# Turning three matrices per group by 32-row blocks through DRAM and VectorE in place of TensorE transposes

## The chip, the cores and the metric

The kernel runs on one core of a Trainium2 chip. The metric is the device time of one execution in microseconds (us). The kernel before takes 2581.26 us, the median of three runs that lie between 2580.55 and 2581.66 us.

## What is computed

The input is x, 128 batches of 128 nodes with 256 features each, in float32, and one 128x128 adjacency matrix. Four layers follow each other, and each has the same frame:

```
h = maximum(layernorm(x), 0)
x = x + layer(h)
```

- Layer 0 is a gated graph layer: `relu((A_in h + e_in)*sigmoid(g_in) + (A_out h + e_out)*sigmoid(g_out) + h*sigmoid(g_loop))`, with gates of one number per node. The kernel gathers the three terms in one 128x128 matrix per batch (`cmb`, the gated sum of A_in, A_out and the identity), which is then multiplied with h.
- Layer 1 is causal attention with one head: scores from h, an additive mask, softmax, product with the values.
- Layer 2 is three graph convolutions, 256 to 512 to 1024 to 256 features.
- Layer 3 is a graph convolution, a product to 512 features, a batch norm over all 128x128 rows, a product back to 256 features, and a second batch norm.

The batch norms need statistics of all rows, so the kernel makes two passes: layers 0 to 2 and the first half of layer 3 for all batches, then the rest of layer 3.

## The kernel before, in words

Four batches form a group (`G = 4`, 512 rows), and there are 32 groups (`NG`). A tile of a group has 128 partitions (the nodes) and the four batches side by side.

The layers are Python generators that yield between stages: `layer0`, `layer1`, `layer2`, `layer3`. The first pass is software-pipelined over groups. In turn g, layer 2 of group g (stream C), layer 1 of group g+1 (stream B), layer 0 of group g+2 (stream A) and layer 3 of group g-1 (stream D) are interleaved, with the norm that opens layer 1 of group g+2 as stream b and that of layer 3 of group g as stream d. The string `TURN` (line 837) says in which order the streams advance; `FINAL` (line 840) does so for the last turn, and `FILL` (line 850) for the start, in which group 0 is worked in halves. A scheduler then places the recorded instructions on the engines; each engine works through its own queue in order and waits where an operand is not there. Loads of x and stores of z go through the SyncE (SP) queue, which also works in order.

TensorE multiplies a stationary operand, contracted over partitions, so some matrices must be turned first. Three matrices of a group are turned by TensorE in the kernel before, each 128x128 block by a multiplication with the identity into PSUM and an eviction to SBUF:

- **cmb** of layer 0, four blocks: the transposes into `pc` on line 553, evicted by VectorE on line 555, used as stationary operand on line 561.
- **h** of layer 1, eight blocks: `turn` (lines 393 to 400), called on line 578, writes two PSUM tiles `pt`; ScalarE evicts the first and VectorE the second into `hT`. `sums` (line 412) then forms combinations of the quarters of hT, and the products of `seven` (line 460, a seven-product scheme for a two-by-two block multiplication) use hT and the sums as operands.
- **p**, the unnormalised softmax of layer 1, four blocks: ScalarE's exponentials on line 649, the transposes into `pp` on line 658, evicted by VectorE on line 660, used as stationary operand for `py` on line 666.

Group 0 and, for layer 0, group 1 take partly different paths at the start (halves, and gates by TensorE), which the change leaves on TensorE.

Of the kernel before, what the change touches and what calls it, by code (L numbers as in the profile page):

```python
# [8 lines left out]
FP = mybir.dt.float32  # L9
AF = mybir.ActivationFunctionType  # L10
ALU = mybir.AluOpType
# [4 lines left out]
P = 128  # L16
# [6 lines left out]
def kernel(  # L23
# [39 lines left out]
    nc = tc.nc  # L63
    B, N, D = x.shape
    G = 4
    NG = B // G
    T = G * N
    DC = D // P
# [13 lines left out]
    def bank(shape, name):  # L82
        return psum[-1].tile(shape, FP, tag="bank", name=name)
# [273 lines left out]
            whole[name] = w.tile(shape, FP, tag=tag, name=name, bufs=bufs)  # L357
        return whole[name]

    def norm(g, layer, bs=ALL):  # L360

        xt, n, tail = X[g], len(bs), f"{layer}_{g}_{bs[0]}"
        st = small.tile([P, n, 6], FP, tag="st", name=f"st{tail}")
        mv = small.tile([P, n, 2], FP, tag="mv", name=f"mv{tail}")
        for k, b in enumerate(bs):
            nc.vector.bn_stats(st[:, k, :], xt[:, b, :])  # L366
        for k in range(n):
            nc.vector.bn_aggr(mv[:, k, :], st[:, k, :])
        rs = small.tile([P, n], FP, tag="rs", name=f"rs{tail}")
        sh = small.tile([P, n], FP, tag="sh", name=f"sh{tail}")  # L370
        if n == G:
            nc.gpsimd.tensor_scalar(rs, mv[:, :, 1], LN_EPS, None, ALU.add)  # L372
            nc.gpsimd.tensor_tensor(rs, rs, nhalf[:, :n], ALU.pow)  # L373
            nc.gpsimd.tensor_scalar(sh, mv[:, :, 0], -1.0, None, ALU.mult)
            nc.gpsimd.tensor_tensor(sh, sh, rs, ALU.mult)  # L375
        else:
            inv_sqrt(rs, mv[:, :, 1], LN_EPS)
            nc.vector.scalar_tensor_tensor(sh, mv[:, :, 0], -1.0, rs, ALU.mult, ALU.mult)
        h = tile_of(g, bs, [P, G, D], "h", f"h{layer}_{g}", 3)
        for k, b in enumerate(bs):  # L380
            relu = nc.scalar.activation(  # L381
                h[:, b, :], xt[:, b, :], AF.Relu, bias=sh[:, k : k + 1], scale=rs[:, k : k + 1]
            )
            if (g, layer) == (1, 0):

                tc.keep_in_program_order(relu)
        return h

    def columns(dst, c, bs):

        return dst[:, c, bs[0] * P : (bs[-1] + 1) * P]

    def turn(dst, h, bs, name):

        for c in range(DC):
            pt = bank([P, len(bs), P], f"{name}_{c}")
            for k, b in enumerate(bs):
                nc.tensor.transpose(pt[:, k, :], h[:, b, c * P : (c + 1) * P], ident)
            evict = nc.vector.tensor_copy if c else nc.scalar.copy
            evict(columns(dst, c, bs), pt.rearrange("p b n -> p (b n)"))  # L400

    def mixed(dst, src, aT, name, evicts, bs=ALL):

# [91 lines left out]
    def layer0(g, bs=ALL):  # L495

        xt, n, tail = X[g], len(bs), f"{g}_{bs[0]}"
        h = norm(g, 0, bs)
        yield
        gl = small.tile([P, n, 3], FP, tag="gl", name=f"gl_{tail}")  # L500
        gate_bias = gb[:, None, :].to_broadcast([P, n, 3])
        if g < 2:

            hT = tile_of(g, bs, [P, DC, T], "dT", f"h0T_{g}", 2)
            turn(hT, h, bs, f"ph_{tail}")
            yield
            pl = bank([P, n, 3], f"pl_{tail}")
            for k, b in enumerate(bs):
                for c in range(DC):
                    nc.tensor.matmul(  # L510
                        pl[:, k, :], hT[:, c, b * P : (b + 1) * P], gwT[:, c, :],
                        start=(c == 0), stop=(c == DC - 1),
                    )
            nc.vector.tensor_tensor(gl, pl, gate_bias, ALU.add)
        else:
            gs = w.tile([P, D], FP, tag="gs", name=f"gs_{tail}", bufs=1)
            for k, b in enumerate(bs):
                for i in range(3):
                    nc.vector.scalar_tensor_tensor(  # L519
                        gs, h[:, b, :], 1.0, gw[:, i, :], ALU.mult, ALU.mult,  # L520
                        accum_out=gl[:, k, i : i + 1],
                    )
                if k == n // 2 - 1:
                    yield
            nc.vector.tensor_tensor(gl, gl, gate_bias, ALU.add)
        gt = small.tile([P, n, 3], FP, tag="gt", name=f"gt_{tail}")
        nc.scalar.activation(gt, gl, AF.Sigmoid)
        yield


        um = tile_of(g, bs, [P, 2, G, D], "um", f"m_{g}", 1)
        bias = um[:, 0]
        cmb, cmbT = (
            um[:, 1, 2 * k : 2 * k + 2, :].rearrange("p a (b n) -> p (a b) n", n=P) for k in range(2)
        )
        for k, b in enumerate(bs):
            nc.scalar.activation(cmb[:, b, :], ain, AF.Copy, scale=gt[:, k, 0:1])
            nc.vector.scalar_tensor_tensor(
                cmb[:, b, :], aout, gt[:, k, 1:2], cmb[:, b, :], ALU.mult, ALU.add
            )  # L540
            nc.vector.scalar_tensor_tensor(
                cmb[:, b, :], ident, gt[:, k, 2:3], cmb[:, b, :], ALU.mult, ALU.add
            )
        for k, b in enumerate(bs):
            nc.scalar.activation(bias[:, b, :], eb, AF.Copy, scale=gt[:, k, 0:1])
        yield
        for k, b in enumerate(bs):
            nc.vector.scalar_tensor_tensor(
                bias[:, b, :], oeb, gt[:, k, 1:2], bias[:, b, :], ALU.mult, ALU.add
            )  # L550
        pc = bank([P, n, P], f"pc_{tail}")
        for k, b in enumerate(bs):
            nc.tensor.transpose(pc[:, k, :], cmb[:, b, :], ident)
        mine = slice(bs[0], bs[-1] + 1)
        nc.vector.tensor_copy(cmbT[:, mine, :], pc)
        yield
        for q in range(bs[0] // 2, (bs[-1] + 1) // 2):
            pm = bank([P, 2, D], f"pm_{g}_{q}")
            for r in range(2):
                b = 2 * q + r  # L560
                nc.tensor.matmul(pm[:, r, :], cmbT[:, b, :], h[:, b, :], start=True, stop=True)  # L561
            half = slice(2 * q, 2 * q + 2)
            nc.vector.tensor_tensor(bias[:, half, :], pm, bias[:, half, :], ALU.add)
        yield
        nc.vector.scalar_tensor_tensor(
            xt[:, mine, :], bias[:, mine, :], 0.0, xt[:, mine, :], ALU.max, ALU.add
        )
        yield

    def layer1(g, bs=ALL):  # L570
# [1 line left out]

        xt, n, tail = X[g], len(bs), f"{g}_{bs[0]}"
        halves = range(bs[0] // 2, (bs[-1] + 1) // 2)
        h = norm(g, 1, bs)
        yield
        hT = tile_of(g, bs, [P, DC, T], "dT", f"hT_{g}", 2)
        turn(hT, h, bs, f"pt_{tail}")
        if n == G:
            ex = w.tile([P, 4, 1, T // 2], FP, tag="ex", name=f"hs_{g}", bufs=2)  # L580
            hs = sums(nc.vector, quarters_t(hT), ex, ex[:, 3])
        yield
# [62 lines left out]
        nmax = small.tile([P, n], FP, tag="nmax", name=f"nmax_{tail}")  # L645
        nc.vector.tensor_reduce(nmax, p, AX.X, ALU.max, negate=True)
        psumr = small.tile([P, n], FP, tag="psumr", name=f"psumr_{tail}")
        for k in range(n):
            nc.scalar.activation(
                p[:, k, :], p[:, k, :], AF.Exp, bias=nmax[:, k : k + 1],  # L650
                accum_out=psumr[:, k : k + 1],
            )
        rsum = small.tile([P, n], FP, tag="rsum", name=f"rsum_{tail}")
        nc.vector.reciprocal(rsum, psumr)
        yield
        pp = bank([P, n, P], f"pp_{tail}")
        for k in range(n):
            nc.tensor.transpose(pp[:, k, :], p[:, k, :], ident)
        pT = tile_of(g, bs, [P, G, P], "pT", f"pT_{g}", 1)[:, bs[0] : bs[-1] + 1, :]
        nc.vector.tensor_copy(pT, pp)  # L660
        yield
        for q in halves:
            py = bank([P, 2, D], f"py_{g}_{q}")
# [109 lines left out]
    def layer3(g):  # L773
# [16 lines left out]
        def put(ij, pb, other):  # L790
# [13 lines left out]
            if done.count(j) == 2:  # L804
                if g < LAST - 1:
                    for jj in range(2):
                        nc.vector.bn_stats(stats1[:, 2 * j + jj, g, :], z[j][:, jj, :])
                if g != LAST:
                    nc.sync.dma_start(Z[g][:, 2 * j : 2 * j + 2, :], z[j])

        if g < LAST:
            yield from seven(columns_by_half(gs, SETS["b"], 0), put, [P, 2, T // 2], f"pz_{g}")
            return
        for i, j in (0, 0), (1, 0), (0, 1), (1, 1):
            pb = bank([P, 2, T // 2], f"pz_{g}_{i}_{j}")
# [18 lines left out]

    TURN = "CCCBCCABBDABBCABBDDCBADCDDBDCCDBACBCCABCCACbBCBBCBCBBCBCBCdB"


    FINAL = "CCCCCCCCCCCCCCCCCCDCCCCDDdDDddDdDdDdddd"  # L840
    US = {}
    AHEAD = 3

# [18 lines left out]
        in_turn(at, KEPT)  # L862
    assert all(next(stream[k], k) == k for k in "acbdA")
    bs, ds = part(layer1, 1), stream["p"]
    next(bs)
    for g in range(NG):
        if g + AHEAD < NG:
            load_x(g + AHEAD)
# [253 lines left out]
```

## Time and profile before

| What | Value | Where it is read |
|---|---|---|
| time | 2581.26 us (2580.55 to 2581.66) | three runs |
| span of the profiled execution | 2581.1 us | page, first line |
| busy TensorE, VectorE, ScalarE, GpSimd | 2535.9, 1905.8, 1288.8, 288.9 us | page, part 1 |
| mean granted TensorE clock | 0.994 | table of cores |
| one turn of the first pass | 70.8 us | the timeline of TensorE: the same block returns every 70.8 us |
| DMA traffic in the first pass | about 31 GB/s, 9% of the engines' time | table of stretches |

The engine columns are busy times, so shares of the span of engines that work beside each other; they do not add up to the span. A TensorE instruction in the timeline overlaps the next one by its pipeline, so what a block of matmuls costs is read as the distance from its start to the start of the block behind it. Float32 matmuls appear as two records each.

### The profile page before, as it was taken

Reading aid. Unit: us, or ns where it says so; the run is one execution under the profiler, and the core shown is the slowest. Engines: PE = TensorE matmul, PEld = TensorE weight load, DVE = VectorE, ACT = ScalarE, POOL = GpSimd, SP = SyncE. Lnnn points to the kernel's source line nnn. Section 1 sums busy time; section 2 is a strip of 40 time slices with the busy share of each in tenths; the row PEclk is TensorE's granted clock in tenths of the full one; section 3 lists DMA queues with packets and bytes.
Section 4 is the critical chain, followed back from the end, with each engine's and each line's share of the span. In section 5 each row is a group of like instructions: output and inputs, shape, how many; then the busy total and the mean of one; then the engine's idle time right before and its main releaser. Section 6 shows DMA issues by size and latency. Waiting matters only on the chain.

```text
span 2581.1 us, 40737 instructions
## 1 busy us (share of the span) xinstructions
PE 2535.9 (98%) x15316; PEld 2293.4 (89%) x15316; DVE 1905.8 (74%) x4795; ACT 1288.8 (50%) x2577; POOL 288.9 (11%) x563
## 2 busy tenths in 40 slices
PE   7999999999999999999999999999999999999996
PEld 6999999999999999999999999999999999988875
DVE  7777777777777777777777777777777777658886
ACT  4545445444444554454444445544454444337766
POOL 1111111111111111011111111110111111000001
PEclk9999999999999999999999999999999999999998
DMA  4000000000000000000000000000100000025459
GB/s 134 15 34 33 34 34 27 24 34 34 34 26 25 34 34 34 34 34 17 34 33 34 33 22 29 34 34 33 34 25 25 34 25 25 25 104 212 173 192 386
DMA packets 49655, 143.05 MB, mean 55 GB/s; under 512 B 4258, under 2 KB 23220, under 8 KB 45492
## 3 DMA queue, kind: packets, MB, share of 16 engines
q1 hardware_dynamic: 42884, 117.33, 12.6%
q0 software_dynamic: 6432, 23.07, 2.5%
q8 instruction: 120, 1.97, 0.3%
q14 instruction: 75, 0.61, 0.1%
q10 hardware_dynamic: 144, 0.07, 0.0%
HBM read 73.48 MB, written 66.98 MB: 54 GB/s over the span
## 4 chain that ended last, share of the span: by engine, by line
PE 95%; ACT 2%; DVE 1%; DMA 1%; issue 0%; POOL 0%; SPq 0%; DVEq 0%; POOLq 0%
PE p_x L452 17%; PE p_x L435 9%; PE p_z L452 8%; PE pmu L407 4%; PE p_z L435 4%; PE p_y L452 4%; PE po_x L995 4%; PE pu_x L435 4%; PE pz_x L452 4%; PE pg L407 2%; PE pm L407 2%; PE ps L636 2%; PE pm L561 2%; PE p_y L435 2%; PE pr L766 2%; PE pqv_x L593 2%
## 5 line engine op out<-in xcount | busy, mean ns | idle before, releaser
L381 ACT ACTIVATE h<-x,sh,rs 128x256 f32<-128x256 f32 x512 | 269.0, 589 | 358.4 <-POOL sh L375 345.8
L452 PE MATMUL p_x<-uT,w 128*128 128x256 f32 x1024 | 242.2, 379 | 0.0
L738 ACT ACTIVATE h2T<-h2T 128x512 f32<-128x512 f32 x192 | 120.5, 627 | 229.9 <-DVE h2T L737 229.9
L452 PEld LDWEIGHTS p_x<-uT,w 128*128 128x128 f32 x1024 | 189.7, 190 | 23.1
L366 DVE BATCH_NORM_STATS2 st<-x 128x6 f32<-128x256 f32 x512 | 190.9, 414 | 2.3
L372 POOL TENSOR_SCALAR rs<-mv 128x4 f32<-128x4 f32 x124 | 29.9, 241 | 1350.0 <-ACT h2T L738 1061.0
L519 DVE SCALAR_TENSOR_TENSOR gs<-h,gw 128x256 f32<-128x256 f32 x360 | 150.4, 418 | 27.9 <-ACT h L381 22.6
L467 ACT COPY p_t<-p_x 128x512 f32<-128x512 f32 (+1 forms) x192 | 96.7, 504 | 109.9 <-PE p_x L452 102.8
L373 POOL TENSOR_TENSOR rs<-rs,nhalf 128x4 f32<-128x4 f32 x124 | 144.6, 1166 | 0.0
L407 PEld LDWEIGHTS pmu<-a2T,u 128*128 128x128 f32 x1024 | 119.3, 192 | 14.8 <-issue 14.8
L435 PEld LDWEIGHTS p_x<-w,h2T 128*128 128x128 f32 x1024 | 124.3, 192 | 3.3
L691 ACT ACTIVATE u<-u 128x512 f32<-128x512 f32 x93 | 58.6, 630 | 133.8 <-DVE u L690 133.8
L435 PE MATMUL p_x<-w,h2T 128*128 128x128 f32 x1024 | 124.6, 275 | 0.0
L452 PE MATMUL p_x<-us,w_s 128*128 128x256 f32 x512 | 121.2, 379 | 0.0
L452 PE MATMUL p_x<-uT,w_s 128*128 128x256 f32 x512 | 121.1, 379 | 0.0
L452 PE MATMUL p_y<-uT,w 128*128 128x256 f32 x512 | 121.0, 379 | 0.0
L452 PE MATMUL p_z<-us,w_s 128*128 128x256 f32 x512 | 121.0, 379 | 0.0
L452 PE MATMUL p_z<-us,w 128*128 128x256 f32 x512 | 120.9, 379 | 0.0
L407 PE MATMUL pmu<-a2T,u 128*128 128x128 f32 x1024 | 119.5, 275 | 0.0
L452 PEld LDWEIGHTS p_z<-us,w_s 128*128 128x128 f32 x512 | 97.3, 190 | 13.2
L452 PEld LDWEIGHTS p_z<-us,w 128*128 128x128 f32 x512 | 97.3, 190 | 13.2
L452 PEld LDWEIGHTS p_y<-uT,w 128*128 128x128 f32 x512 | 97.2, 190 | 13.2
(324 smaller groups left out, 6115.6 us busy)
## 6 DMA issues: line engine op xcount, KB each, us to landing
z<-zo SPq DMA_DIRECT2D x62, 512.0 KB, 2.6
zi<-z SPq DMA_DIRECT2D x31, 1024.0 KB, 4.9
x<-x POOLq DMA_DIRECT2D x32, 512.0 KB, 3.5
x<-in_x_dram SPq DMA_DIRECT2D x31, 512.0 KB, 4.0
out_dram<-x3i SPq DMA_DIRECT2D x30, 512.0 KB, 10.7
x3i<-x SPq DMA_DIRECT2D x20, 512.0 KB, 6.1
x3i<-x POOLq DMA_DIRECT2D x12, 512.0 KB, 8.8
w<-in_L_gnn_W_dram SPq DMA_DIRECT2D x1, 2048.0 KB
```

What stands on the lines that cost most here:

```text
L366: nc.vector.bn_stats(st[:, k, :], xt[:, b, :])
L373: nc.gpsimd.tensor_tensor(rs, rs, nhalf[:, :n], ALU.pow)
L381: relu = nc.scalar.activation(h[:, b, :], xt[:, b, :], AF.Relu, bias=sh[:, k : k + 1], scale=rs[:, k : k + 1])
L407: nc.tensor.matmul(pm[:, k, :], src[:, b, c * P : (c + 1) * P], aT, start=True, stop=True)
L435: nc.tensor.matmul(pb[:, rr, :], a_r[r][:, c, rr * P : (rr + 1) * P], b_r[r][:, c, :wide], start=(first and rr == 0 and c == 0), stop=(c = ...
L452: nc.tensor.matmul(pb[:, jj, :], b_r[r][:, c, at : at + P], a_r[r][:, c, :], start=(first and jj == 0 and c == 0), stop=(c == nk - 1), ski ...
L467: nc.scalar.copy(t, pb)
L519: nc.vector.scalar_tensor_tensor(gs, h[:, b, :], 1.0, gw[:, i, :], ALU.mult, ALU.mult, accum_out=gl[:, k, i : i + 1],)
L561: nc.tensor.matmul(pm[:, r, :], cmbT[:, b, :], h[:, b, :], start=True, stop=True)
L691: nc.scalar.activation(dst, dst, AF.Relu)
L738: nc.scalar.activation(dst, dst, AF.Relu)
L995: nc.tensor.matmul(pb, BW2R[r][:, c, :], a_r[r][:, c, :], start=(first and c == 0), stop=(c == FC // 2 - 1), skip_group_check=True,)
```

## The change

The three matrices are no longer turned by TensorE. A 128x128 block is seen as four by four blocks of 32x32. Turning it is an exchange of those blocks across the diagonal, and a turn inside each block. The exchange is done by DMA: four writes, one for each stripe of 32 partitions, put the blocks into a DRAM tile `home` in exchanged order, and one read brings them back (`swap`). The turn inside the blocks is one VectorE instruction over all blocks (`cut`).

So that each piece that travels is contiguous, the instruction that makes the matrix (ScalarE's relu for h, VectorE's last addition for cmb, ScalarE's exponential for p) writes it already in a blocked layout. The purpose is to take the transposes off TensorE's queue. Since an exchange takes longer than a transpose, the streams get more yields between making and using a turned matrix, and `TURN` is rewritten so that other work stands between them. The stores of z are moved behind the exchange reads of the turn in the SP queue (`follow`).

It applies to cmb of groups 2 to 31, and to h and p of groups 1 to 31.

```diff
@@ norm @@
         for k, b in enumerate(bs):
+            dst, src = h[:, b, :], xt[:, b, :]
+            if blocks:
+                dst = h.rearrange("p b d -> p (b d)").rearrange(
+                    "p (j k b r) -> p b j k r", j=P // 32, k=DC, b=G
+                )[:, b]
+                src = src.rearrange("p (k j r) -> p j k r", k=DC, j=P // 32)
             relu = nc.scalar.activation(
-                h[:, b, :], xt[:, b, :], AF.Relu, bias=sh[:, k : k + 1], scale=rs[:, k : k + 1]
+                dst, src, AF.Relu, bias=sh[:, k : k + 1], scale=rs[:, k : k + 1]
             )
...
+    def swap(blocks, name):
+        e = blocks.shape[1] // NQ
+        home = scratch.tile([NQ, Q, NQ, e], FP, name=name)
+        for i in range(NQ):
+            nc.sync.dma_start(
+                home[:, :, i, :].rearrange("j r e -> r j e"),
+                blocks[i * Q : (i + 1) * Q].rearrange("p (j e) -> p j e", j=NQ),
+            )
+        nc.sync.dma_start(blocks, home.rearrange("j r i e -> (j r) (i e)"))
+        fetched.append(nc.cur_bb.bb.instructions[-1].name)
+
+    def cut(dst, blocks, nb):
+        tc.keep_in_program_order(
+            nc.vector.transpose(
+                dst.rearrange("p (b i c) -> p b i c", b=nb, i=NQ),
+                blocks.rearrange("p (i b c) -> p b i c", i=NQ, b=nb),
+            )
+        )
@@ layer0 @@
-            nc.vector.scalar_tensor_tensor(
-                cmb[:, b, :], ident, gt[:, k, 2:3], cmb[:, b, :], ALU.mult, ALU.add
-            )
+            dst, one, now = cmb[:, b, :], ident, cmb[:, b, :]
+            if g >= 2:
+                dst = flatT.rearrange("p (j b r) -> p b j r", j=NQ, b=G)[:, b]
+                one, now = (a.rearrange("p (j r) -> p j r", j=NQ) for a in (one, now))
+            nc.vector.scalar_tensor_tensor(dst, one, gt[:, k, 2:3], now, ALU.mult, ALU.add)
+        if g >= 2:
+            swap(flatT, f"cc_{g}")
...
-        pc = bank([P, n, P], f"pc_{tail}")
-        for k, b in enumerate(bs):
-            nc.tensor.transpose(pc[:, k, :], cmb[:, b, :], ident)
         mine = slice(bs[0], bs[-1] + 1)
-        nc.vector.tensor_copy(cmbT[:, mine, :], pc)
+        if g >= 2:
+            yield
+            cut(cmb.rearrange("p b n -> p (b n)"), flatT, G)
+            cmbT = cmb
+        else:
...
@@ layer1 @@
-        h = norm(g, 1, bs)
+        h = norm(g, 1, bs, n == G)
+        if n == G:
+            blocks = h.rearrange("p b d -> p (b d)")
+            swap(blocks, f"hc_{g}")
         yield
         hT = tile_of(g, bs, [P, DC, T], "dT", f"hT_{g}", 2)
-        turn(hT, h, bs, f"pt_{tail}")
-        if n == G:
+        if n < G:
+            turn(hT, h, bs, f"pt_{tail}")
+        else:
+            cut(hT.rearrange("p c t -> p (c t)"), blocks, DC * G)
+            yield
             ex = w.tile([P, 4, 1, T // 2], FP, tag="ex", name=f"hs_{g}", bufs=2)
             hs = sums(nc.vector, quarters_t(hT), ex, ex[:, 3])
...
+        if n == G:
+            swap(flat_p, f"pc_{g}")
...
-        pp = bank([P, n, P], f"pp_{tail}")
-        for k in range(n):
-            nc.tensor.transpose(pp[:, k, :], p[:, k, :], ident)
-        pT = tile_of(g, bs, [P, G, P], "pT", f"pT_{g}", 1)[:, bs[0] : bs[-1] + 1, :]
-        nc.vector.tensor_copy(pT, pp)
+        if n == G:
+            cut(p.rearrange("p b s -> p (b s)"), flat_p, G)
+            pT = p
+        else:
...
@@ layer3 @@
-                if g != LAST:
-                    nc.sync.dma_start(Z[g][:, 2 * j : 2 * j + 2, :], z[j])
...
+            at = len(nc.cur_bb.bb.instructions)
+            for j in (1, 0):
+                nc.sync.dma_start(Z[g][:, 2 * j : 2 * j + 2, :], z[j])
+            for i in nc.cur_bb.bb.instructions[at:]:
+                for name in fetched[-2:]:
+                    follow(i, name)
+            yield
...
-    TURN = "CCCBCCABBDABBCABBDDCBADCDDBDCCDBACBCCABCCACbBCBBCBCBBCBCBCdB"
+    TURN = "CCBBCBCABCBBCABDBACBDDACDCADDCDCBDCADBCBACACbCBCBBCBBCBBCBCbBCd"
-    FINAL = "CCCCCCCCCCCCCCCCCCDCCCCDDdDDddDdDdDdddd"
+    FINAL = "CCCCCCCCCCCCCCCCCCDCCCCDDdDDddDdDdDDdddd"
...
-    next(bs)
+    for _ in range(2):
+        next(bs)
```

More of the change, by code (lines that the diff above doesn't have):

```diff
@@ L358, in tile_of, with norm @@
         return whole[name]
-    def norm(g, layer, bs=ALL):
+    def norm(g, layer, bs=ALL, blocks=False):
         xt, n, tail = X[g], len(bs), f"{layer}_{g}_{bs[0]}"
@@ L400, in turn, with follow @@
             evict(columns(dst, c, bs), pt.rearrange("p b n -> p (b n)"))
+    Q = 32
+    NQ = P // Q
+    fetched = []
+    def follow(i, name):
+        tc.add_manual_dep(
+            i, name,
+            mybir.DependencyInfo(mybir.DependencyClass.NoSync, mybir.DependencyReason.DATA),
+            reason="follow",
+        )
[15 more added lines that the diff above has]
+            )
+        )
     def mixed(dst, src, aT, name, evicts, bs=ALL):
@@ L535, in layer0 @@
         )
+        flatT = cmbT.rearrange("p b n -> p (b n)")
         for k, b in enumerate(bs):
@@ L550, in layer0 @@
             )
-        pc = bank([P, n, P], f"pc_{tail}")
-        for k, b in enumerate(bs):
-            nc.tensor.transpose(pc[:, k, :], cmb[:, b, :], ident)
         mine = slice(bs[0], bs[-1] + 1)
-        nc.vector.tensor_copy(cmbT[:, mine, :], pc)
+        if g >= 2:
[3 more added lines that the diff above has]
+        else:
+            pc = bank([P, n, P], f"pc_{tail}")
+            for k, b in enumerate(bs):
+                nc.tensor.transpose(pc[:, k, :], cmb[:, b, :], ident)
+            nc.vector.tensor_copy(cmbT[:, mine, :], pc)
         yield
@@ L647, in layer1 @@
         psumr = small.tile([P, n], FP, tag="psumr", name=f"psumr_{tail}")
+        pT = tile_of(g, bs, [P, G, P], "pT", f"pT_{g}", 1)[:, bs[0] : bs[-1] + 1, :]
+        flat_p = pT.rearrange("p b s -> p (b s)")
         for k in range(n):
+            dst, src = p[:, k, :], p[:, k, :]
+            if n == G:
+                dst = flat_p.rearrange("p (j b r) -> p b j r", j=NQ, b=G)[:, k]
+                src = src.rearrange("p (j r) -> p j r", j=NQ)
             nc.scalar.activation(
-                p[:, k, :], p[:, k, :], AF.Exp, bias=nmax[:, k : k + 1],
-                accum_out=psumr[:, k : k + 1],
-            )
+                dst, src, AF.Exp, bias=nmax[:, k : k + 1], accum_out=psumr[:, k : k + 1],
+            )
+        if n == G:
+            swap(flat_p, f"pc_{g}")
         rsum = small.tile([P, n], FP, tag="rsum", name=f"rsum_{tail}")
@@ L655, in layer1 @@
         yield
-        pp = bank([P, n, P], f"pp_{tail}")
-        for k in range(n):
-            nc.tensor.transpose(pp[:, k, :], p[:, k, :], ident)
-        pT = tile_of(g, bs, [P, G, P], "pT", f"pT_{g}", 1)[:, bs[0] : bs[-1] + 1, :]
-        nc.vector.tensor_copy(pT, pp)
+        if n == G:
+            cut(p.rearrange("p b s -> p (b s)"), flat_p, G)
+            pT = p
+        else:
+            pp = bank([P, n, P], f"pp_{tail}")
+            for k in range(n):
+                nc.tensor.transpose(pp[:, k, :], p[:, k, :], ident)
+            nc.vector.tensor_copy(pT, pp)
         yield
```

## The prediction

> **What bounds the kernel now.** I read the table of stretches first: how busy each engine is in one turn of the first pass, at what clock, with how much DMA. Three of its rows (length, then busy time and instructions of TensorE, its weight loads, VectorE, ScalarE, GpSimd, then clock, DMA share, GB/s):
>
> ```profile
> 978.80:1049.60 70.80, 70.80 (x440) 64.53 (x439) 52.77 (x138) 34.45 (x70) 8.68 (x17) 1.00 0.09 31
> 1049.60:1120.40 70.80, 70.80 (x440) 64.53 (x439) 52.78 (x138) 34.45 (x70) 8.68 (x17) 1.00 0.09 30
> 1120.40:1191.20 70.80, 70.80 (x440) 64.53 (x439) 52.77 (x138) 34.44 (x70) 8.69 (x17) 1.00 0.09 31
> ```
>
> TensorE fills every turn to the last hundredth at full clock, VectorE is idle for 18 us of it, ScalarE for 36 us, DMA nearly always. The page's chain of waits agrees for the whole span:
>
> ```profile
> PE 95%; ACT 2%; DVE 1%; DMA 1%; issue 0%; POOL 0%; SPq 0%; DVEq 0%; POOLq 0%
> ```
>
> So TensorE time removed in the steady state shortens the kernel one for one, as long as nothing that TensorE needs comes later than its turn in the queue. Busy time of a transpose is not its price, since neighbours overlap; the timeline of TensorE gives the price as the distance between starts:
>
> ```profile
> 1016.20 0.60 PE L658 MATMUL pp<-ident,p 128*128 128x128 f32 x4
> 1016.64 0.60 PE L553 MATMUL pc<-ident,m 128*128 128x128 f32 x4
> 1017.07 1.89 PE L452 MATMUL p_x<-us,w_s 128*128 128x256 f32 x8
> ...
> 1058.27 1.04 PE L398 MATMUL pt<-ident,h 128*128 128x128 f32 x8
> 1059.14 1.89 PE L452 MATMUL p_x<-us,w_s 128*128 128x256 f32 x8
> ```
>
> Four transposes of p and four of cmb take 1017.07-1016.20 = 0.87 us, eight of h 0.87 us, with no bracket of idle time behind any of them.
>
> [...]no turn by VectorE is in this trace. [...]a z store of 512 KB lands in 2.6 us, an x load of 512 KB in 4.1 us[...]. The trace shows the slowing after an even shorter gap, in the fill:
>
> ```profile
> 29.54 0.33 PE L398 MATMUL pt<-ident,h 128*128 128x128 f32 x1 [1.47 <-ACT h L381]
> 30.03 0.90 PE L398 MATMUL pt<-ident,h 128*128 128x128 f32 x3 [0.16 <-ACT h L381]
> 30.97 2.08 PE L612 MATMUL pqv<-hT,m_qk 128*128 128x256 f32 x4
> 32.84 1.27 PE L620 MATMUL pqv<-w_vo,hT 128*128 128x128 f32 x8
> 33.94 1.03 PE L612 MATMUL pqv<-hT,m_qk 128*128 128x256 f32 x4
> ```
>
> The same four records take 2.08 us at first and 1.03 us later. From 29.54 to 32.84 passed 3.3 us where 1.3 us of work at full rate and 0.2 us of waiting stood: 1.8 us lost.
>
> **What is removed.** h and p in 31 groups, 31 x (0.87+0.435) = 40.5 us, and cmb in 30 groups, 30 x 0.435 = 13.0 us: **-53.5 us**, 1.74 us a turn. With them go evictions of 0.69+0.69+0.68 us on VectorE and 0.59 us on ScalarE per turn.
>
> **What is added beside TensorE.** On VectorE one block turn of 128x1024 and two of 128x512. Nearest rows of those sizes: 1.23 us (the addition on L565) and 0.69 us (the eviction on L660), together 2.6 us, net +0.5 us in 18 us of idle time. At twice the price it is +3.2 us, still within it. ScalarE and VectorE write h, p and cmb in runs of 32 elements; I take the time as unchanged, since both have idle time. DMA: 2 MB more per turn, beside the 2.2 MB of now (31 GB/s x 70.8 us): a share of 0.09 becomes about 0.17. SP's queue gets 15 more issues of 0.32 to 0.38 us, 5.7 us in a queue that had three.
>
> **The new waits.** Each block turn waits on VectorE for its read, the read waits on SP for its four writes, and what is queued behind on either waits too. I count where the turned matrix is used in the order in which the built changed kernel's instructions stand on each engine (no time is in that order; every time is from the trace of before). Times below run from the event named, and one matmul of 128x256 counts 0.433 us (a block of four: 1018.80-1017.07 = 1.73).
>
> *p*: between the end of the scores `ps` and the first `py` stand seven pz blocks of two matmuls and 21 matmuls of layer 2: 35 x 0.433 = 15.2 us. The chain: the mask and the maximum, with a zo addition between them that waits for pz_y (1.73 us), done at 1.73+0.69+0.69 = 3.1; four exponentials, whose starts lie 0.39 us apart (1012.66 to 1013.83 in the timeline of ScalarE, ending 0.4 later): 4.8; four writes behind those of cmb on SP: last issued near 6.0; landed by 8.6 if they need the 2.6 us of a z store; read landed by 12.7 if it needs the 4.1 us of an x load; turned by 13.4. Slack 1.8 us, with sizes two to eight times too large on the DMA side. Behind it on VectorE stands an addition whose product ends only just before py.
>
> *cmb*: read issued one place ahead of p's, turned just after it (14.1), used after py, at 18.6 us at the earliest.
>
> *h*: its relu ends 0.3 us after pu_x starts in the trace of before (1034.85 and 1034.58). Writes landed by 4.4, read landed by 8.5. VectorE reaches the turn only after an addition whose product ends at 10.6 us by the same count, so it finds the data there. It ends by 11.9; the uT copies behind it wait for a product that ends at 14.1, and `pqv` follows only at 22.
>
> So in the steady state I put the cost at zero; what hides it is the 15.2 and 22 us of other matmuls.
>
> **The fill is different.** For group 1 the h exchange has no turn of work ahead of it. Before:
>
> ```profile
> 67.12 2.07 ACT L381 ACTIVATE h<-x,sh,rs 128x256 f32<-128x256 f32 x4
> ...
> 69.72 1.99 PE L452 MATMUL p_x<-uT,w 128*128 128x256 f32 x8
> ...
> 75.01 1.04 PE L398 MATMUL pt<-ident,h 128*128 128x128 f32 x8
> ```
>
> In the changed order TensorE goes from p_x at 69.72 through twelve matmuls (5.2 us, to 74.9) straight to the first product with hT. That h is ready at 69.2; its exchange, behind 0.9 MB of weight stores on the same queue, would land near 79. But VectorE's turn also stands behind twelve gate products `gs` (0.42+0.06 us each, some 5.8 us), three small ones (1 us) from about 74.2, then the gates' sigmoid and the first cmb additions, which put it near 83; it ends near 84.3. TensorE would idle from 74.9 to 84.3, **+9.4 us**, and restart at half rate, **+1.8 us** as above. If the scheduler's queue is less bad than I count, the bound below is landing time plus turn, 80.2 or +5.3; above, with a slow read, +12.
>
> **Sum.** 2581.3 - 53.5 + 9.4 + 1.8 = **2539 us**.
>
> **Rivals.**
> 1. The steady state as above and the fill hidden too: 2581.3-53.5 = 2528. Against it: the order of VectorE's queue. Chance 0.1.
> 2. The exchange is partly exposed: the p turn comes 1 us after its deadline, each turn loses 1 us, 2539+31 = 2570. For it: a slack of only 1.8 us, a transfer in 512-byte pieces that this trace shows only as a small load, and two reads at once. Against: I priced small transfers as large ones. Chance 0.12.
> 3. Slower: a hop takes 3 us more than priced each, or VectorE, blocked at a turn, holds back evictions that TensorE waits for. Stalls of 3 us beyond the deadline in 31 turns cost 93 us, 2539+93 = 2632. For it: in-order queues, where one late read holds three engines. Against: VectorE idles 18 us a turn, and h has over 2 us of room before it holds anything. Chance 0.08.
>
> **How the numbers follow.** The forecast has 0.68, and a case between rivals 2 and 3 that lands on no change 0.02. Faster: 0.68+0.1+0.12 = 0.90; same 0.02; slower 0.08. The range runs from rival 1's 2527 to rival 2's 2570, which leaves out rival 3, no change and the worse half of rival 2, under 2 in 10.
>
> **What would show it.** Right: a turn of 69.06 us with TensorE at 70.80-1.74 busy and no idle bracket at py, pm or pqv; one gap of about 9 us before the first pqv near 75 us; clock 1.00. Wrong: idle time of TensorE before L731 in every turn, put down to a VectorE turn, itself put down to a DMA (rivals 2 and 3); a granted clock below 1.00 in the turns; a block turn far over 1.2 us.

## The result and the profile after

The changed kernel takes **2627.14 us** (median of four runs, 2626.43 to 2627.78) beside 2581.46 us for the kernel before on the same chip: a ratio of 1.0175, 95% interval 1.0161 to 1.0189. It is 45.7 us slower, where 2539 us had been predicted.

The page's chain of waits, shares by engine, shows at once that TensorE no longer sets the end alone. Before it had 95% of the chain:

```profile
PE 52%; DVE 21%; issue 11%; ACT 10%; POOL 4%; DMA 0%; SPq 0%; DVEq 0%; ACTq 0%; POOLq 0%
```

DMA has 0%, although three exchanges per turn were added. VectorE, ScalarE and GpSimd together have 35%. The table of stretches for one turn (length; busy TensorE, weight loads, VectorE, ScalarE, GpSimd; clock, DMA share, GB/s) says how much a turn lost:

```profile
1078.08:1149.71 71.63, 70.19 (x425) 63.16 (x423) 53.71 (x137) 33.12 (x69) 8.00 (x17) 1.00 0.20 59
```

The granted clock is 1.00. The turn was to be 69.06 us and is 71.63: **2.57 us a turn**, about 77 us in 30 turns, against 53.5 us taken off TensorE. TensorE's waits for the whole span (waiting instruction and line, what it waited for; us in total, times, longest) name the places:

```profile
PE pu_x L474 <- DVE mT L449: 34.8, 30, 1.2
PE pqv_x L643 <- DVE hT L435: 8.6, 1, 8.6
...
PE pqv_x L643 <- DVE qv L658: 6.1, 28, 0.4
```

The second is the gap of the fill that was predicted. The first comes in every turn and has nothing to do with a turned matrix: `mT` is the operand of layer 2's first product, made after the norm that follows the attention. Distances between starts in one turn give the whole 2.6 us: 1.4 at pu_x (1.3 before it, 0.1 because it then runs slower itself), 0.5 before `pqv_x` with m_qk_s, 0.3 around `pqv_z`, and about 0.1 at each of four other places.

The block turns themselves (line 435; duration min/median/max, first and last start), and how long VectorE stood idle before any of them in the whole run (the profile calls the matrix cmb `m`):

```profile
L435 DVE STREAM_TRANSPOSE hT<-h x31: 1233/1234/1246, 82.4 to 2218.7; 128x1024 f32<-128x1024 f32 x31
L435 DVE STREAM_TRANSPOSE p<-pT x31: 694/694/714, 112.3 to 2260.6; 128x512 f32<-128x512 f32 x31
...
  DMA h<-hc: 2.8, 5
```

VectorE waited for an exchange for only 2.8 us in 2627, and for h alone. And the transfers (KB each, median us from issue to landing):

```profile
h<-hc SPq DMA_DIRECT2D x31, 512.0 KB, 3.5
pc<-pT SPq DMA_DIRECT2D x124, 64.0 KB, 1.8
pT<-pc SPq DMA_DIRECT2D x31, 256.0 KB, 2.9
```

All are shorter than they were priced. So the exchange through DRAM landed in time, and the question is why mT did not.

**How mT came late.** TensorE, VectorE and ScalarE in one turn, from the timeline (start, length, engine, line, result and operands, idle time and what ended it):

```profile
1046.19 1.97 PE L731 MATMUL py<-qv,p 128*128 128x256 f32 x8
...
1058.10 1.95 PE L474 MATMUL p_z<-w_s,h2s 128*128 128x128 f32 x16
1061.21 1.13 PE L474 MATMUL pu_x<-w,mT 128*128 128x256 f32 x4 [1.17 <-DVE mT L449]
```

```profile
1047.13 0.70 DVE L435 STREAM_TRANSPOSE m<-m 128x512 f32<-128x512 f32 x1
1047.75 1.61 DVE L734 SCALAR_TENSOR_TENSOR x<-py,rsum,x 128x256 f32<-128x256 f32 x4
...
1057.14 0.69 DVE L457 TENSOR_TENSOR h2s<-h2T 128x512 f32<-128x512 f32 x1 [1.83 <-ACT h2T L795]
...
1060.48 0.68 DVE L449 COPY mT<-pm 128x512 f32<-128x512 f32 x1
```

```profile
1054.29 2.07 ACT L387 ACTIVATE h<-x,sh,rs 128x256 f32<-128x256 f32 x4 [3.45 <-POOL sh L375]
...
1056.52 0.59 ACT L795 ACTIVATE h2T<-p_x 128x512 f32<-128x512 f32 x1
```

The chain begins at `py`. VectorE adds py into x (1047.75), but m's block turn stands in front of that addition. Statistics, GpSimd and ScalarE's four norm activations follow (1054.29). The relu that completes h2T, an operand of layer 2 of the group ahead, stands behind these on ScalarE (1056.52), VectorE idles 1.83 us for it, and mT's eviction stands behind the h2s sums that need it (1060.48). From py to pu_x passed 15.02 us. The kernel before had the same chain, and TensorE and VectorE came to its end so:

```profile
1018.80 1.89 PE L666 MATMUL py<-qv,pT 128*128 128x256 f32 x8
...
1034.58 1.03 PE L435 MATMUL pu_x<-w,mT 128*128 128x256 f32 x4
```

```profile
1032.93 0.68 DVE L410 COPY mT<-pm 128x512 f32<-128x512 f32 x1
```

TensorE's own work between the two was 15.78 us there, and mT's eviction began 14.13 us after py: this work was the cover of the chain, and it was enough. In the changed kernel the work is 13.7 us (15.02 less the 1.33 us lost before pu_x), and the eviction begins 14.29 us after py. The chain is hardly longer than before; its cover is 2.1 us shorter.

VectorE took its queue in order, and that made mT late. It idled 1.83 us for h2T while the last of four statistics of the next group's x, complete since 1054.20, stood behind; that one ran at 1057.75. And pm, the product that mT evicts, was started at 1056.31, and ScalarE's half of the eviction began at 1058.30; VectorE's half began only at 1060.48, 2.18 us later, behind sums that have nothing to do with it. The experiments below close the gap before pu_x with no buffer added.

**The fill.** The first gap was predicted as 9.4 us and 1.8 us for the restart. The second was not foreseen:

```profile
83.78 1.19 PE L643 MATMUL pqv_x<-hT,m_qk 128*128 128x256 f32 x2 [8.57 <-DVE hT L435]
...
123.72 3.74 PE L446 MATMUL pm<-a2T,h 128*128 128x128 f32 x16 [2.47 <-ACT h L387]
127.25 2.74 PE L474 MATMUL p_z<-w_s,h2s 128*128 128x128 f32 x16
```

8.6 us of gap and 2.1 of restart at the first, 2.5 and 2.5 at the second (the last two blocks take 3.53 and 2.58 us from start to start instead of 1.79). The sum: 2581.5 - 53.5 + 77 + 10.7 + 5.0 = 2621 us. The other 6 us were not traced one by one; some of them belong to the fill of the new order itself, whose first `pr` (layer 2's last product) starts at 131.59 us in order_only (below), with no exchange, and at 127.50 us in the kernel before.

### The profile page after: what moved, and what is told of

It reads as the page before. It is cut to its first block, busy times and chain, and to the rows that moved or that the text cites. A ratio compares the mean times of both kernels' runs of the same rounds, so it can differ in the third digit from the quotient of the medians.

```text
span 2625.7 us, 40828 instructions
## 1 busy us (share of the span) xinstructions
PE 2524.2 (96%) x14824; PEld 2255.9 (86%) x14824; DVE 1934.7 (74%) x4795; ACT 1248.9 (48%) x2546; POOL 269.1 (10%) x563
## 4 chain that ended last, share of the span: by engine, by line
PE 52%; DVE 21%; issue 11%; ACT 10%; POOL 4%; DMA 0%; SPq 0%; DVEq 0%; ACTq 0%; POOLq 0%
PE p_x L491 9%; PE p_x L474 7%; ACT h L387 5%; PE p_z L491 5%; PE pu_x L474 4%; PE pmu L446 4%; DVE gs L558 4%; PE pz_x L491 4%; DVE st L366 3%; PE p_z L474 2%; PE p_y L491 2%; DVE h2T L802 2%; POOL rs L373 2%; PE py L731 2%; PE ps L691 2%
## 5 line engine op out<-in xcount | busy, mean ns | idle before, releaser
L491 PE MATMUL p_x<-uT,w 128*128 128x256 f32 x1024 | 247.5, 380 | 0.0
L366 DVE BATCH_NORM_STATS2 st<-x 128x6 f32<-128x256 f32 x512 | 182.5, 411 | 1.2
L373 POOL TENSOR_TENSOR rs<-rs,nhalf 128x4 f32<-128x4 f32 x124 | 128.5, 1037 | 0.0
L491 PE MATMUL p_z<-us,w_s 128*128 128x256 f32 x512 | 126.9, 382 | 0.0
L449 DVE COPY uT<-pmu 128x512 f32<-128x512 f32 (+1 forms) x132 | 88.2, 672 | 36.6 <-PE pmu L446 36.4
## 6 DMA issues: line engine op xcount, KB each, us to landing
out_dram<-x3i SPq DMA_DIRECT2D x30, 512.0 KB, 10.7
```

Source lines behind the costliest of these rows:

```text
L449: evicts[c % len(evicts)](columns(dst, c, bs), pm.rearrange("p b n -> p (b n)"))
L491: nc.tensor.matmul(pb[:, jj, :], b_r[r][:, c, at : at + P], a_r[r][:, c, :], start=(first and jj == 0 and c == 0), stop=(c == nk - 1), ski ...
```

## The experiments

Theory A: the exchange is hidden, and the new order of the streams moved other waits past the point where TensorE wants them. Rival B: the latency of the exchange through DRAM holds the engines. Rival C: VectorE, with the block turns, is too full.

| Kernel | Time, us | Before beside it, us | Ratio, 95% interval | One turn, us |
|---|---|---|---|---|
| order_only | 2622.78 | 2582.94 | 1.0154, 1.0139 to 1.0169 | 72.0 |
| exch_old_order | 2704.64 | 2582.94 | 1.0473, 1.0455 to 1.0490 | 73.4 to 75.0 |
| mt_act | 2620.11 | 2582.94 | 1.0143, 1.0128 to 1.0158 | 71.5 |
| no_wait | 2642.93 | 2582.94 | 1.0230, 1.0215 to 1.0245 | 72.3 to 74.0 |
| no_cc | 2620.27 | 2583.17 | 1.0143, 1.0128 to 1.0159 | 71.4 |
| two_hops | 2700.78 | 2583.17 | 1.0456, 1.0438 to 1.0473 | 73.6 to 74.3 |
| one_letter | 2607.29 | 2583.55 | 1.0093, 1.0078 to 1.0108 | 71.1 |
| three_letters | 2555.31 | 2583.55 | 0.9889, 0.9874 to 0.9904 | 69.4 |
| three_letters_tensore | 2608.58 | 2583.55 | 1.0098, 1.0081 to 1.0114 | 71.6 to 72.0 |
| first_h | 2546.73 | 2583.22 | 0.9858, 0.9845 to 0.9872 | 69.4 |
| best | 2535.83 | 2583.22 | 0.9819, 0.9806 to 0.9832 | 69.06 |

### The order without the exchange, the exchange without the order

order_only keeps TURN, FINAL and the extra steps of the changed kernel and turns all three matrices by TensorE, as before:

```diff
-            cut(cmb.rearrange("p b n -> p (b n)"), flatT, G)
+            pc = bank([P, n, P], f"pc_{tail}")
...
-            cut(hT.rearrange("p c t -> p (c t)"), blocks, DC * G)
+            turn(hT, h, bs, f"pt_{tail}")
...
-            cut(p.rearrange("p b s -> p (b s)"), flat_p, G)
+            pp = bank([P, n, P], f"pp_{tail}")
```

> The new order of the streams and the extra steps stay, but all three matrices are turned by TensorE as before, with no exchange through DRAM. Theory A (the new order moves waits that have nothing to do with the exchange, above all mT before pu_x and the norm chain behind it, past the point where TensorE wants them): slower than before, 2600 to 2660 us, a turn of 71.5 to 73 us against 70.8, and TensorE idle before pu_x on mT. Rival B (the exchange and its block turns hold the engines, the order is harmless): 2575 to 2590 us, the turn within 0.2 us of before's 70.8, no idle time before pu_x.

exch_old_order does the reverse; the added steps are gone with the order:

```diff
-    TURN = "CCBBCBCABCBBCABDBACBDDACDCADDCDCBDCADBCBACACbCBCBBCBBCBBCBCbBCd"
+    TURN = "CCCBCCABBDABBCABBDDCBADCDDBDCCDBACBCCABCCACbBCBBCBCBBCBCBCdB"
-    FINAL = "CCCCCCCCCCCCCCCCCCDCCCCDDdDDddDdDdDDdddd"
+    FINAL = "CCCCCCCCCCCCCCCCCCDCCCCDDdDDddDdDdDdddd"
```

> The exchange stays, but the order of the streams is the one of the kernel before (TURN and FINAL, no extra steps, the z writes still after the exchange's reads). Theory A (the exchange needs a new order, since in the old one each turned matrix is wanted before it has come back; the price was paid for in other waits): slower than the changed kernel, 2630 to 2690 us, with the idle time of TensorE now on the block turns (before pm, pqv_x or py). Rival B (the exchange is cheap anywhere and the new order alone costs): 2525 to 2560 us, no idle time on block turns.

order_only took 2622.78 us: **the new order alone costs 40 us**, with no exchange in the kernel. Rival B's 2575 to 2590 fails. But the detail of theory A fails too: TensorE waited only once on mT before pu_x. What it lost lies around pqv_x, pqv_z and p_z, about 1.2 us a turn. Removing the transposes, 1.74 us of TensorE time a turn, bought only 0.37 us a turn in this order (72.00 us with them, 71.63 without), and the fill took more than that back: the first `pr` starts at 131.59 us with them and at 146.59 without. Why the wait before pu_x came with the exchange, two lines of TensorE and one of VectorE in order_only show:

```profile
1035.87 1.89 PE L717 MATMUL py<-qv,pT 128*128 128x256 f32 x8
...
1049.93 1.05 PE L474 MATMUL pu_x<-w,mT 128*128 128x256 f32 x4
```

```profile
1049.12 0.68 DVE L449 COPY mT<-pm 128x512 f32<-128x512 f32 x1
```

From py to pu_x TensorE has 14.06 us of work, and mT's eviction begins 13.25 us after py, just in time. So the new order alone took 1.7 of the 2.1 us of cover. With the exchange the eviction begins 14.29 us after py, and the work is 0.4 us less. About half of that delay arises before the addition into x, where VectorE is later behind py; the rest are statistics of the next norm that stand among the h2s sums.

exch_old_order took 2704.64 us, slower than theory A's 2690. The exchange does need another order, but not for the reason that I gave. TensorE never waits for a block turn. TensorE's largest wait, and VectorE's idle time before its block turns:

```profile
PE pm L446 <- ACT h L387: 63.5, 31, 3.6
```

```profile
  DMA m<-cc: 5.6, 8
```

It is the norm behind py again: its h comes 2 us too late in each turn. TURN is that of the kernel before, but the scheduler's queue for TensorE is not: nearly three blocks of layer 2, 4.75 us, that stood behind py there stand ahead of it here. Between py and pm TensorE has 7.5 us of work, where it had 12.2 before (1018.80 to 1031.01). The exchange got its room ahead of py, and the chain behind py lost it.

### mT evicted by ScalarE

```diff
-        mixed(mT, h, a2T, f"pm2_{tail}", (nc.vector.tensor_copy, nc.scalar.copy), bs)
+        mixed(mT, h, a2T, f"pm2_{tail}", (nc.scalar.copy,), bs)
```

> The changed kernel, with both halves of mT evicted by ScalarE instead of one by VectorE and one by ScalarE. Theory A (mT's first eviction stands in VectorE's queue behind the h2s sums, which wait for ScalarE): the 43 us before pu_x fall to under 10, some of it comes back elsewhere because ScalarE has 0.7 us more to do; 2590 to 2612 us. Rival B (DRAM latency of the exchange sets the turn): 2622 to 2632 us, as the changed kernel. Rival C (VectorE as a whole is too full): some gain, as VectorE loses 0.7 us a turn, at most 0.7 x 30 = 21 us, so 2606 or more.

The wait on VectorE's mT is gone, from py to pu_x TensorE runs without a gap (13.69 us), and the kernel gains only 7 us. The time stands a few products further on; TensorE's wait, and two lines of ScalarE's timeline:

```profile
PE pu_x L474 <- ACT pu_t L506: 28.9, 29, 1.0
```

```profile
1061.89 2.07 ACT L387 ACTIVATE h<-x,sh,rs 128x256 f32<-128x256 f32 x4 [3.68 <-POOL sh L375]
1064.12 0.57 ACT L506 COPY pu_t<-pu_x 128x512 f32<-128x512 f32 x1
```

That is the product of pu_x with ms. It waits for the eviction `pu_t`, which stands on ScalarE behind the four activations of another norm, and ScalarE idles 3.68 us for that norm's numbers from GpSimd. mT's evictions were done long before (1058.2). Theory A was right on the place and wrong on the size, which lies in rival C's range; between A and C this run does not decide.

### No block turn waits for its read

```diff
-        nc.sync.dma_start(blocks, home.rearrange("j r i e -> (j r) (i e)"))
+        sink = scratch.tile([NQ * Q, NQ * e], FP, name=f"{name}_sink")
+        nc.sync.dma_start(sink, home.rearrange("j r i e -> (j r) (i e)"))
```

> The changed kernel with the same bytes in the same transfers, but the read of each exchange goes to another place in DRAM, so no block turn waits for a read (the turned matrices then hold blocks that have not been exchanged). Theory A (the exchange lands in time): 2605 to 2635 us, a turn of 70.9 or more, with the idle time before pu_x still there. Rival B (the wait for the exchange is what cost): the turn falls to 69.1 to 69.5, 2545 to 2565 us.

2642.93 us: **no theory foresaw that taking the wait away makes it 16 us slower**. With one dependency fewer the queues are laid out anew. ScalarE now has the norm that opens a later group's layer 1 in front of the second half of mT, and TensorE waits for that half at pu_y; two lines of ScalarE's timeline, and one of TensorE's:

```profile
1060.82 2.07 ACT L387 ACTIVATE h<-x,sh,rs 128x256 f32<-128x256 f32 x4 [3.86 <-POOL sh L375]
1062.80 0.56 ACT L450 COPY mT<-pm 128x512 f32<-128x512 f32 x1
```

```profile
1063.41 1.13 PE L475 MATMUL pu_y<-w,mT 128*128 128x256 f32 x4 [1.68 <-ACT mT L450]
```

So the run is no clean measure of the wait alone. It does show that rival B's gain is not to be had by removing the wait.

### m turned by TensorE, and one more hop

no_cc takes one of the three exchanges out:

```diff
-            if g >= 2:
+            if False:
...
-        if g >= 2:
-            swap(flatT, f"cc_{g}")
...
-            cut(cmb.rearrange("p b n -> p (b n)"), flatT, G)
-            cmbT = cmb
-        else:
+        if True:
             pc = bank([P, n, P], f"pc_{tail}")
```

> The changed kernel with cmb turned by TensorE again (no exchange and no block turn for it), the order and the other two exchanges as they are. Theory A (what makes TensorE idle before pu_x is a chain of VectorE and ScalarE steps that starts at py; m's block turn stands in it between py and the sums into x): TensorE has 0.43 us a turn more to do, and the chain is 0.6 us shorter, so the 1.33 us before pu_x falls by 0.6 to 1.33 us a turn; 2600 to 2622 us. Rival B (DRAM latency or the load on the transfers sets the turn): no change or slower by the 13 us of TensorE's work, 2625 to 2642 us.

```profile
1056.69 1.95 PE L474 MATMUL p_z<-w_s,h2s 128*128 128x128 f32 x16
1059.17 1.13 PE L474 MATMUL pu_x<-w,mT 128*128 128x256 f32 x4 [0.53 <-DVE mT L449]
```

The distance is 2.48 us where the block takes 1.79: 0.69 us lost instead of 1.32. TensorE has 0.43 us a turn more to do, and still the kernel gains 7 us. In place of the block turn VectorE has an eviction of the same length (0.68 us), so the chain is little shorter: from py to pu_x passed 14.81 us instead of 15.02. Most of the gain there is cover. The transposes stand ahead of py, and two products of p_x have moved from there to behind py, so TensorE's work between py and pu_x is 14.12 us instead of 13.69. The time is within theory A's range and outside rival B's. This bears out that the chain from py sets the turn, not which of its members costs what.

two_hops puts one more copy into each exchange:

```diff
-        nc.sync.dma_start(blocks, home.rearrange("j r i e -> (j r) (i e)"))
+        again = scratch.tile([NQ * Q, NQ * e], FP, name=f"{name}_again")
+        nc.sync.dma_start(again, home.rearrange("j r i e -> (j r) (i e)"))
+        nc.sync.dma_start(blocks, again)
```

> The changed kernel with one more copy through DRAM in each of the three exchanges. Theory A (the exchanges land in time, with about 1.8 us to spare for p and more for h and m): one more hop of 4 to 5 us takes up the slack and exposes 2 to 4 us a turn, 2685 to 2750 us, with TensorE now idle at py or the block turn of p the longest wait of VectorE. Rival B (the exchange already holds the turn): all of the hop is exposed for at least one matrix, and the two others lengthen the same chain, 2760 us or more.

2700.78 us, within theory A's range and below rival B's. But py waited only 5.1 us in the whole run, and VectorE idled 8 us in all before its block turns. The queues were laid out anew here too, with the block turns later, and TensorE's waits are on p_t, mT and h2T. The slack of the exchange was therefore not measured by this run.

### One letter, with TensorE's queue unchanged

```diff
-    TURN = "CCBBCBCABCBBCABDBACBDDACDCADDCDCBDCADBCBACACbCBCBBCBBCBBCBCbBCd"
+    TURN = "CCBBCBCABCBBCABDBACBDDACDCADDCDCBDCADBCBAACbCCBCBBCBBCBBCBCbBCd"
```

> The changed kernel with one letter of TURN moved three places on (one step of layer2, C). TensorE's instructions keep exactly the same order; what changes is the order of a few instructions in the queues of VectorE and ScalarE around the norm of the next group and mT. Theory A (what was lost stands in the order of VectorE's and ScalarE's queues): the idle time before pu_x changes by some 0.6 us a turn, so the whole by 10 to 25 us, 2602 to 2617 us if it goes the right way. Rival B (DRAM latency or the load of the transfers): all transfers and block turns stay as they are, so within 4 us of 2627. Rival C (VectorE has too much to do): its work is the same, so within 4 us of 2627.

```profile
1050.93 1.95 PE L474 MATMUL p_z<-w_s,h2s 128*128 128x128 f32 x16
1053.46 1.13 PE L474 MATMUL pu_x<-w,mT 128*128 128x256 f32 x4 [0.59 <-DVE mT L449]
```

**20 us faster**, and 0.74 us lost before pu_x instead of 1.32. TensorE's queue is the same instruction for instruction, and so are the transfers. On VectorE the last statistics of the next group's norm now run in the idle time ahead of the h2s sums and no longer between these and mT. From the first h2s sum to mT's eviction pass 2.75 us (1049.98 to 1052.73) instead of 3.34 (1057.14 to 1060.48). B and C, which had nothing changed, foresaw 2623 to 2631.

### Three letters, with the exchange and without

```diff
-    TURN = "CCBBCBCABCBBCABDBACBDDACDCADDCDCBDCADBCBACACbCBCBBCBBCBBCBCbBCd"
+    TURN = "CCBBCBCABCBBCABDACBDBDACDCADDCDCBDCADBCBAACbCCBCBBCBBCBBCBCbCdB"
```

> The changed kernel with three letters of TURN moved: one step of layer2 (C) three places on, one of layer1 (B, the turn of u) past layer2's last step and the z writes, one of layer1 (B, ps) four places on. The exchange, the block turns, the amount of work of each engine and the transfers stay. Theory A (the order of the steps, not the exchange, lost the time): most of the 2.6 us a turn comes back, 2545 to 2580 us, below the kernel before. Rival B (the exchange through DRAM cannot be hidden in this kernel) and rival C (VectorE too full): 2610 us or more, since neither changes.

three_letters_tensore has this TURN and turns all three matrices by TensorE, with the edit of order_only.

> The order of the run before this one (three letters moved), with all three matrices turned by TensorE and no exchange. Theory A (in an order that leaves no other wait, the exchange is worth what it takes off TensorE, at most 53.5 us): 40 to 70 us slower than the run with the exchange, 2600 to 2635 us. Rival (the three letters bring the gain whatever turns the matrices): as fast as the run with the exchange or faster.

2555.31 us with the exchange, 2608.58 without: **with the same TURN the exchange is worth 53.3 us**. That this is so near to the 53.5 us of the removed transposes is a coincidence. In the turns it gains more than their 1.74 us, 2.23 us (71.60 against 69.37), since the run with transposes has a wait of its own:

```profile
PE pqv_x L634 <- ACT pqv_t L506: 16.3, 29, 0.9
```

In the fill it loses: the first `pr` starts at 128.89 us with the transposes and at 141.74 with the exchange. The exchange kernel is below the kernel before, and with the same exchange, block turns and amount of work it is 72 us below the changed kernel. B and C both fall. The order alone, with TensorE's transposes, is no gain: 2608.58 against 2583.55.

### The first exchange, and the best order found

```diff
-        h = norm(g, 1, bs, n == G)
-        if n == G:
+        far = n == G and g > 1
+        h = norm(g, 1, bs, far)
+        if far:
...
-        if n < G:
+        if not far:
             turn(hT, h, bs, f"pt_{tail}")
```

> The order with three letters moved, and h of group 1 turned by TensorE; all later groups as before. Theory A (in the fill nothing else is ready for TensorE while group 1's h is exchanged, so this one exchange is exposed): the 8.7 us before the first pqv and the half rate after it go, against 1.3 us more for TensorE, so 7 to 12 us less than with the three letters alone: 2543 to 2549 us. Rival (the gap is only the first of several, and TensorE then waits for the next matrix of the fill instead): within 3 us of 2555.

2546.73 us, 8.6 us less than three_letters, as theory A had it. On top of it, more letters moved:

```diff
-    TURN = "CCBBCBCABCBBCABDACBDBDACDCADDCDCBDCADBCBAACbCCBCBBCBBCBBCBCbCdB"
+    TURN = "CBCBCBABCBCBCABDACDBBDACDCADDCDCBDCADBCBAACbCCBCCBBBCBBCCBbBCdB"
```

> As the run before it, with some more letters of TURN moved, so that mT comes a little earlier still. Theory A: the 0.25 us before pu_x and the two restarts of 0.1 us of each turn go, 8 to 12 us in all, 2533 to 2541 us, that is the kernel before less about 45 us, and what remains is TensorE's own work. Rival (other waits of the same size take their place): within 4 us of the run before it.

**2535.83 us**, 0.9819 of the kernel before (0.9806 to 0.9832), faster than both kernels. The table of stretches, the chain of waits and TensorE's timeline of this kernel:

```profile
959.14:1028.20 69.06, 69.06 (x423) 63.05 (x422) 53.80 (x138) 33.41 (x69) 8.00 (x17) 1.00 0.20 62
```

```profile
PE 94%; DVE 2%; DMA 2%; ACT 1%; issue 0%; POOL 0%; SPq 0%; DVEq 0%; POOLq 0%; ACTq 0%
```

```profile
1000.96 1.89 PE L733 MATMUL py<-qv,p 128*128 128x256 f32 x8
...
1015.01 1.95 PE L474 MATMUL p_x<-w_s,h2s 128*128 128x128 f32 x16
1016.80 1.03 PE L474 MATMUL pu_x<-w,mT 128*128 128x256 f32 x4
```

The turn is 69.06 us and TensorE is busy for all of it; VectorE works as long as in the changed kernel (53.80 against 53.71 us). A whole block of layer 2 (p_x with h2s, 1.79 us) now stands ahead of pu_x, and from py to pu_x are 15.84 us of TensorE's own work. The cover that the kernel before had (15.78 us) is back.

## Why the prediction was wrong, step by step

- **What bounds the kernel, and what is removed: right.** 1.74 us a turn were summed, and in best, where TensorE is busy for the whole of the turn shown, that turn is 69.06 us instead of 70.80. The 53.3 us of three_letters against three_letters_tensore agree with the sum of 53.5 by luck, as said there.
- **What is added beside TensorE: nearly right, and harmless.** The block turns were put at 1.23 and 0.69 us, an estimate from other instructions of those sizes, and took 1.23 and 0.69 to 0.70. VectorE's turn rose by 0.9 us (0.5 predicted), DMA's share to 0.20 (0.17). SP's fifteen issues took 2.99 + 1.93 + 1.77 us for the writes and 0.34 for each read, 7.7 us (5.7). The 4.1 us taken for an x load are 4.0 on the page of before.
- **The new waits of p, cmb and h: right in outcome.** In the turn shown, p's block turn ran from 1045.35 to 1046.04 and py started at 1046.19; TensorE lost 0.1 us there. But p's chain was mis-sized: from the end of `ps` (1030.97) it took 15.1 us, not 13.4, so of the 1.8 us of slack 0.15 were left. SP had the last of p's writes issued 9.3 us after `ps`, not 6.0, behind the 2.99 us of cmb's, and the block turn stood behind statistics on VectorE. VectorE's idle time for the exchange was 2.8 us in all.
- **"So in the steady state I put the cost at zero": the step that failed.** It should have been 2.57 us a turn, 77 us. I counted deadlines for the three turned matrices alone. The diff also rewrote TURN and added steps, and I read that as room for the exchange, at no price. It changes when every other operand is wanted and what stands ahead of it in two in-order queues. The wait that costs most, pu_x on mT, appears nowhere in the prediction; its room could have been counted from the trace of before, where mT's eviction begins 14.13 us after py, against 13.7 us of work from py to pu_x in the new order.
- **The fill: right for the gap foreseen** (8.6 us and 2.1 against 9.4 and 1.8), and short by a second gap of 2.5 us with a restart of 2.5.
- **The rivals.** The third lies within 5 us of what was measured, by accident: it had the hops or a VectorE blocked at a block turn as its cause, and neither was there; an eviction was held back, but by sums that waited for ScalarE. Of the signs that were to show the prediction wrong none appeared; the idle time came before line 474, which was not on the list.

What is shown: the time in the turns was lost to where steps stand in the queues, and not to transfers that came late. With the same exchange, block turns and amount of work, the order alone decides whether the kernel is 46 us slower than before or 28 us faster (three_letters), and one_letter gains 20 us of that with TensorE's queue unchanged. Of the 2.57 us a turn, 1.2 came with the new order alone (order_only) and the other 1.4 only with the exchange in that order. What stays open: the slack of the exchange, which no run measured alone; the share of each member in the chain from py; and some 6 us of the ledger.

## What to carry to other kernels

When TensorE is full, its work is also the cover of every chain on the other engines; before taking work away, count for each operand that TensorE waits for, not only for those the change touches, how much of its queue lies between the start of the chain and its use. A change that rewrites the order of the work should be measured in two halves, the order alone and the mechanism with the order held fixed: here +40 us for the order alone, and for the mechanism +4 us in that order and -53 us in a better one. Room made ahead of one product is taken from what stands behind it, so it has a price too. After a change of latency, search the order again before judging the mechanism.

## What the runs showed of the hardware that was not expected

- How long a gap slows TensorE afterwards. Gaps of 1.17 us and of 1.68 us in full turns cost 0.1 us more at the restart, the first product after the gap. The 1.8 us that the prediction put down to a gap of 1.47 us in the fill came after other gaps (0.52 us before the product at 26.94), so the length of one gap does not settle it. In exch_old_order a gap of 2.04 us was followed by two blocks at less than two thirds of the rate:

```profile
1013.13 3.11 PE L446 MATMUL pm<-a2T,h 128*128 128x128 f32 x16 [2.04 <-ACT h L387]
1016.03 3.15 PE L474 MATMUL p_z<-w_s,h2s 128*128 128x128 f32 x16
1019.02 1.06 PE L474 MATMUL p_x<-w_s,h2s 128*128 128x128 f32 x8
```

  They take 2.90 and 2.99 us from start to start instead of 1.79, so the restart cost 2.3 us, more than the gap, and the mean granted clock of this kernel was 0.977 against 0.991 of the changed kernel.
- In the changed kernel the exchange's smaller transfers were quicker than its larger ones, and its reads quicker than the 4.1 us at which I priced them: writes of 64 KB landed in 1.8 us and of 128 KB in 2.5, reads of 256 KB in 2.7 to 2.9 and of 512 KB in 3.5 us.
- Writing in runs of 32 elements cost ScalarE's exponentials nothing: one of 128x128 took 386 ns in the blocked layout and 387 ns in the plain one.
